# Graph layer with residual normalisation: single normalisation steps, the first x load on SyncE's queue, and evictions planned 0.3 later

## The chip, the cores and the metric

The kernel runs on one core of one Trainium2 chip. The metric is the device time of that core in microseconds; lower is better. Each kernel is executed several times and the median is taken. One more execution is recorded by the hardware profiler, and every duration of a single instruction below comes from that one.

## The reference, cut to what matters

There are 6250 nodes with 128 features and 100000 edges, sorted by destination. Every edge has one of two types. The layer multiplies the source node's features by the weights of the edge's type, sums over the edges that end in a node, adds the node's own product, applies relu, adds the input and normalises each row.

```python
Xs = X[src]
m_data = Xs @ W_data.T + b_data
m_ctrl = Xs @ W_control.T + b_control
msg = jnp.where((edge_types == 0)[:, None], m_data, m_ctrl)
agg = jax.ops.segment_sum(msg, dst, num_segments=X.shape[0])
out = agg + (X @ W_self.T + b_self)
h = x + relu(out)
result = (h - mean(h)) / sqrt(var(h) + 1e-5)      # along each row
```

## The kernel before, in words

The 6250 nodes are cut into 49 blocks of 128. In the first stage, called the y stage here, TensorE multiplies each block by both edge weights (the name y) and adds the bias with a second matmul. The result is kept as three bf16 parts, so that later bf16 matmuls lose nothing: ScalarE copies the first part out of PSUM into m3, TensorE subtracts it from y by a matmul with minus the identity, ScalarE copies the second part, and so on (the steps yh, y1, ym, y2, yl). The parts also go to a table in device memory. At the same time the edges of each destination block are loaded through a window that begins at the block's first edge. To find those first edges, VectorE compares the first destinations of rows of edges (r0, begun), GpSimd gathers one row per block (er), and TensorE turns the counts into a row (the matmul at L355), from which SyncE takes its addresses (first).

After that, 35 blocks are summed by matmuls and 14 by indirect gathers. For the 35, edges are put into slots by ranks (matmuls called tri and rest, reductions called slot, and the fill matmuls that write the tile small). The slots of a block go to device memory (packed) and come back broadcast to all partitions (rows); VectorE turns rows into one-hot matrices. Then, for each of 25 tiles of a block, four matmuls gather 128 edge messages into a PSUM tile g_ps (step g), ScalarE evicts it to gs in bf16 (step e), and four matmuls sum it into the block's agg with another one-hot matrix hot_d (step s). There are four g_ps buffers and eight gs buffers, so step g of a tile also waits for the eviction four tiles earlier. The last tile of a block goes to mixed, whose first rows come by an indirect gather. In the last group of blocks, VectorE may take an eviction instead of ScalarE. For the other 14 blocks, GpSimd gathers rows of the table (msg), and matmuls sum them with the one-hot matrix hot_g.

A finished block gets its own product (step o), relu, the residual and row statistics on VectorE. Blocks are then normalised in groups of up to five: VectorE and ScalarE compute scale and shift, and ScalarE applies them with one activation per block (L190, the function apply). The result is stored.

The order of all this on every engine is not left to the hardware. Each stage is a generator of steps; a step has a name, a cost for each engine that may run it, the names it needs, and a lag. The class Order runs them all against planned clocks, one per engine (T for TensorE, V, A, G and S for VectorE, ScalarE, GpSimd and SyncE). It picks the engine that can start first, and among the steps that could start there within 0.1 us the one with the earliest due time. A step's end is its start plus cost plus lag, and what needs it may start 0.25 later:

```python
self.free[engine] = start + costs[engine]
self.end[name] = start + costs[engine] + lag
```

The instructions are emitted in that order, and each engine runs its queue in order, with semaphores for what a step really needs. So costs, lags, due times and the initial clocks in order.free (L296) change no wait, only the order of the queues. The due times come from LEAD, BUILT, BLOCK and PACE (L383).

The head of the program, ahead of the planned steps, is written in a fixed order: the load of r0 on SyncE's queue, the loads of the bias and of w_sb on ScalarE's queue, constants, the bias split into three parts on VectorE (L271 to L274) and copied by ScalarE to bias3 (L276), then r0f and begun. A last branch, sums_over_all, is a fallback that is entered only if the windows missed edges.

Of the kernel before, what the change touches and what calls it, by code (L numbers as in the profile page):

```python
# [9 lines left out]
F32 = mybir.dt.float32  # L10
BF16 = mybir.dt.bfloat16
I32 = mybir.dt.int32
AF = mybir.ActivationFunctionType
# [6 lines left out]
P = 128  # L20
D = 128
D3 = 3 * D
# [29 lines left out]
PARTS = (4, 8, 8, 8, 8, 8, 5)  # L52
# [48 lines left out]
def step(name, costs, *needs, lag=0.0):  # L101
    return as_tuple(name), costs, [as_tuple(n) for n in needs], lag
# [6 lines left out]
@with_exitstack  # L109
def kernel(  # L110
    ctx: ExitStack,
    tc: tile.TileContext,
    x: bass.AP,
    xt: bass.AP,
    edges: bass.AP,
    w: bass.AP,
    bias: bass.AP,
    out: bass.AP,
):

    nc = tc.nc  # L140
    dram = ctx.enter_context(tc.tile_pool(name="dram", bufs=1, space=DRAM))
    const = ctx.enter_context(tc.tile_pool(name="const", bufs=1))
    table = dram.tile([NT * P, D3], BF16, name="table")
    packed = dram.tile([NPB, NT * R], BF16, name="packed")
    total = const.tile([1, 1], I32, name="total")

    def finish(h, agg, xs):

        nc.vector.scalar_tensor_tensor(h, agg, 0.0, xs, op0=ALU.max, op1=ALU.add)

    def add_parts(agg, work):
        whole = work.tile([P, D], F32, name="whole")
        nc.vector.tensor_reduce(whole, agg.rearrange("p (i c) -> p c i", i=3), axis=AX.X, op=ALU.add)  # L153
        return whole

    def load_rows(b, work, name="xs", bufs=2):
        xs = work.tile([P, D], F32, name=name, bufs=bufs)
        nc.sync.dma_start(xs, x[b * P : (b + 1) * P, :])
        return xs

    def stats(mv, h, work):
        st = work.tile([P, 6], F32, name="st")
        nc.vector.bn_stats(st, h)
        nc.vector.bn_aggr(mv, st)

    def root(mv, n, work):
        v = work.tile([P, Q], F32, name="v")
        nc.vector.tensor_scalar_add(v[:, :n], mv[:, :n, 1], EPS)
        s0 = work.tile([P, Q], F32, name="s0")
        nc.scalar.activation(s0[:, :n], v[:, :n], AF.Sqrt)  # L170
        return v, s0

    def scale(mv, v, s0, n, work):

        r0 = work.tile([P, Q], F32, name="r0")
        nc.vector.reciprocal(r0[:, :n], s0[:, :n])
        q = work.tile([P, Q], F32, name="q")
        nc.vector.tensor_mul(q[:, :n], v[:, :n], r0[:, :n])
        nc.vector.tensor_add(q[:, :n], q[:, :n], s0[:, :n])
        rstd = work.tile([P, Q], F32, name="rstd")  # L180
        nc.vector.reciprocal(rstd[:, :n], q[:, :n])
        nc.vector.tensor_scalar_mul(rstd[:, :n], rstd[:, :n], 2.0)
        shift = work.tile([P, Q], F32, name="shift")
        nc.vector.scalar_tensor_tensor(shift[:, :n], mv[:, :n, 0], -1.0, rstd[:, :n],
                                       op0=ALU.mult, op1=ALU.mult)
        return rstd, shift

    def apply(h, rstd, shift, n):
        for j in range(n):
            nc.scalar.activation(h[:, j, :], h[:, j, :], AF.Identity,  # L190
                                 bias=shift[:, j : j + 1], scale=rstd[:, j : j + 1])

    def store_out(h, b0, n, by=nc.sync):
        n0 = b0 * P
        full = min(n, (N - n0) // P)
        if full:
            by.dma_start(
                out[n0 : n0 + full * P, :].rearrange("(b p) f -> p b f", p=P), h[:, :full, :]
            )
        if full < n:  # L200
            n1 = n0 + full * P
            nc.sync.dma_start(out[n1:N, :], h[: N - n1, full, :])

    norm = stats, root, scale, apply, store_out

    with ExitStack() as main:
        sums_over_windows(main, tc, x, xt, edges, w, bias, table, packed, total,
                          add_parts, finish, load_rows, norm)

    matched = nc.values_load(total[0:1, 0:1])  # L210
    with tc.If(matched != E), ExitStack() as rest:
        sums_over_all(rest, tc, xt, edges, w, bias, table, dram, finish, load_rows, norm)


def sums_over_windows(ctx, tc, x, xt, edges, w, bias, table, packed, total,
# [21 lines left out]
    early = ctx.enter_context(ExitStack())  # L237
    build = early.enter_context(tc.tile_pool(name="build", bufs=2))
    ps_y = early.enter_context(tc.tile_pool(name="ps_y", bufs=YB, space=PSUM))
    b1 = build.tile([1, D3], F32, name="b1", bufs=1)  # L240
    A.dma_start(b1, bias)
    w_sb = const.tile([D, D3], F32, name="w_sb")
    A.dma_start(w_sb, w)


    iota_f = const.tile([P, 640], F32, name="iota_f")
# [46 lines left out]
        in_offset=bass.IndirectOffsetOnAxis(ap=row_i[:, 0:1], axis=0),  # L293
    )

    order.free.update(V=7.0, T=6.5, G=8.0)  # L296


    pid1 = const.tile([P, 1], F32, name="pid1")
# [74 lines left out]
            )  # L374


    xts, ys = {}, {}
    at_part = [sum(PARTS[:g]) for g in range(len(PARTS))]
    two_blocks = [(g, b, min(2, at_part[g] + n - b))
                  for g, n in enumerate(PARTS) for b in range(at_part[g], at_part[g] + n, 2)]  # L380


    LEAD, BUILT = 8.0, 76  # L383
    BLOCK = 13.1
    PACE = 1.68
    AHEAD, FIRST = 26.0, 20
# [60 lines left out]
    def load_x():  # L447
        for g, n in enumerate(PARTS):
            free = [("y", at_part[g - 1] - 1)] if g > 1 else []
            yield step(("xt", g), {"A": 0.45}, *free, lag=3.5)  # L450
            xts[g] = build.tile([D, max(PARTS), P], F32, name="xt")[:, :n]
            A.dma_start(xts[g].rearrange("p b c -> p (b c)"),
                        xt[:, at_part[g] * P : (at_part[g] + n) * P])

    def multiply():
        for i, (g, b, n) in enumerate(two_blocks):
            for j in range(n):
                free = [("yl", two_blocks[i - YB][1])] if i >= YB and j == 0 else []
                yield step(("y", b + j), {"T": 0.97}, ("xt", g), *free)
                if j == 0:  # L460
                    y = ys[b] = ps_y.tile([P, 2, 2 * D], F32, name="y")
                T.matmul(y[:, j, :], xts[g][:, b + j - at_part[g], :], w_sb[:, : 2 * D],  # L462
                         start=j == 0, stop=False, skip_group_check=True)
                T.matmul(y[:, j, :], ones_b, bias3[:, : 2 * D], start=False, stop=True, skip_group_check=True)  # L464
# [294 lines left out]
    def evict():  # L759
        for i, (b, g) in enumerate(tiles):  # L760
            free = [("s", *tiles[i - EB])] if i >= EB else []
            if g == NS - 1 and b:
                free.append(("s", b - 1, g))
            costs = {"A": 0.37, "V": 0.53} if b >= STARTS[-1] else {"A": 0.37}
            e = yield step(("e", b, g), costs, ("g", b, g), *free)
            if g < NS - 1:
                gs, at = late.tile([P, D3], BF16, name="gs", bufs=EB), slice(P)
            else:
                gs, at = mixed[blocks[b][0] % 2], slice(2 * R, P)
            gs_tiles[b, g] = gs  # L770
            (A.copy if e == "A" else V.tensor_copy)(gs[at], g_tiles.pop((b, g))[at, :D3])  # L771
# [19 lines left out]
    def own_of(blocks, begun):  # L791

        for i, b in enumerate(blocks):
            yield step(("agg", b), {"S": 0.0}, *([("whole", blocks[i - 1])] if i else []))
            yield step(("o", b), {"T": 0.5}, ("xs", b), begun(b))
            by_columns(aggs[b][:, :D], x_ts.pop(b), w_sb[:, 2 * D :], start=False, stop=False,
                       skip_group_check=True)
            by_columns(aggs[b][:, :D], ones_b, bias3[:, 2 * D :], start=False, stop=False,
                       skip_group_check=True)
# [16 lines left out]
    def normalise(pieces, last):  # L816

        for grp, (get, b0, q0, n) in enumerate(pieces):
            yield step((last, "root", grp), {"V": 0.2}, ("sum", b0 + n - 1))
            h, mv = get()  # L820
            h, mv = h[:, q0 : q0 + n, :], mv[:, q0 : q0 + n, :]
            v, s0 = root(mv, n, work)
            yield step((last, "rooted", grp), {"A": 0.3}, (last, "root", grp))
            yield step((last, "scale", grp), {"V": 1.0}, (last, "rooted", grp))
            scales = scale(mv, v, s0, n, work)
            yield step((last, "apply", grp), {"A": 0.28 * n}, (last, "scale", grp))
            apply(h, *scales, n)
            at_end = last == "p" and grp == len(pieces) - 1
            yield step((last, "out", grp), {"A": 0.4} if at_end else {"S": 0.3}, (last, "apply", grp))
            store_out(h, b0, n, nc.scalar if at_end else nc.sync)  # L830


# [99 lines left out]
def sums_over_all(ctx, tc, xt, edges, w, bias, table, dram, finish, load_rows, norm):  # L932
# [69 lines left out]
    for b0 in range(0, NB, Q):  # L1002
# [12 lines left out]
            finish(h[:, j, :], s_in, load_rows(b0 + j, work))  # L1015
            stats(mv[:, j, :], h[:, j, :], work)
        v, s0 = root(mv, n, work)
        apply(h, *scale(mv, v, s0, n, work), n)
        store_out(h, b0, n)


# [29 lines left out]
```

## Time and profile before

| What | Value |
|---|---|
| Median of 3 runs | 545.55 us (544.28 to 546.7) |
| The profiled execution | 628.27 us, its span 626.6 us |
| TensorE matmul busy | 550.4 us, 88% of the span |
| VectorE busy | 429.4 us, 69% |
| ScalarE busy | 424.7 us, 68% |
| GpSimd busy | 292.8 us, 47% |
| Mean granted TensorE clock | 0.985 |
| One eviction gs<-g_ps on ScalarE | 494 ns, 804 of them |
| One apply on ScalarE | 497 ns, 49 of them |

The profiled execution is slower than the runs without a profiler, so its durations and waits are compared with each other and with its own time. A line such as "PE agg L232 <- ACT gs L771" means that TensorE, at line 232, writing agg, sat idle until ScalarE's instruction at line 771 that wrote gs had ended. In a timeline line the first number is the start, the second the duration, both in us, then engine, line, operation, output and inputs, and in brackets the idle time before it and what ended it. "PE" is a matmul, "PEld" a weight load, "ACTq" and "SPq" are DMA issues in the queues of ScalarE and SyncE.

### The profile page before, as it was taken

The page shows a single profiled execution, that of the slowest core. Times are in us where ns is not written, and L with a number is a line of the kernel's source. Part 1 is how long each engine was busy: PE and PEld are TensorE (multiplying, and loading weights), DVE is VectorE, ACT ScalarE, POOL GpSimd, SP SyncE. Part 2 cuts the span into 40 slices and gives each one's busy share as a digit, 9 for nine tenths or more (in the row PEclk, how much of TensorE's full clock was granted, in tenths as well). Part 3 has the DMA queues.
Part 4 walks back from the last instruction along what each step waited for, and adds up shares of the span by engine and source line. Part 5 has one row for each costly group of instructions (what it writes and reads, how often), then busy time and mean ns, then how long its engine had stood idle before and what let it go on. Part 6 is the DMA issues. An engine that isn't in the chain of part 4 may idle for free.

```text
span 626.6 us, 26397 instructions
## 1 busy us (share of the span) xinstructions
PE 550.4 (88%) x11222; PEld 441.2 (70%) x11222; DVE 429.4 (69%) x962; ACT 424.7 (68%) x1008; POOL 292.8 (47%) x267
## 2 busy tenths in 40 slices
PE   5899888896989898897988989999999998888994
PEld 3555466675768686786877877788777787666783
DVE  4767677567667777776787766877686667446784
ACT  6755555565587666777767676786767876676684
POOL 1000026654465556655556464665646554554400
PEclk9999988999899999999999999999999999999998
DMA  3567754324243433435333433443344542534300
GB/s 108 168 196 221 249 188 128 117 66 158 58 127 123 127 111 117 136 109 152 93 128 114 142 122 106 127 144 106 122 133 119 157 152 68 161 103 146 106 18 27
DMA packets 60932, 79.19 MB, mean 126 GB/s; under 512 B 15760, under 2 KB 51371, under 8 KB 60807
## 3 DMA queue, kind: packets, MB, share of 16 engines
q1 hardware_dynamic: 47109, 48.88, 24.3%
q0 software_dynamic: 12400, 25.08, 14.3%
q10 hardware_dynamic: 1298, 3.48, 1.6%
q8 instruction: 89, 1.46, 0.9%
q14 instruction: 36, 0.29, 0.1%
HBM read 64.35 MB, written 13.05 MB: 124 GB/s over the span
## 4 chain that ended last, share of the span: by engine, by line
PE 80%; ACT 7%; issue 5%; DVE 4%; DMA 2%; SPq 1%; another core or an unknown queue 0%; POOL 0%; ACTq 0%; DVEq 0%; POOLq 0%
PE agg L232 27%; PE g_ps L756 26%; PE acc L232 8%; PE agg_g L232 8%; PE small L602 7%; ACT gs L771 5%; PE y L462 2%; ACT h_p L190 1%; DMA rows<-packed 1%; DVE slot L565 1%; PE y L480 1%; DVE hot_st L548 1%; ACT h_g L190 1%; PE y L464 0%; DMA xt<-in_xt 0%
## 5 line engine op out<-in xcount | busy, mean ns | idle before, releaser
L771 ACT CAST gs<-g_ps 128x384 bf16<-128x384 f32 x804 | 337.2, 494 | 151.3 <-PE g_ps L756 97.4
L857 POOL DMA_INDIRECT msg<-table,idx x252 | 283.1, 1124 | 208.0 <-PE g_ps L756 90.5
L756 PE MATMUL g_ps<-m,rows 128*32 128x384 bf16 x3430 | 330.8, 334 | 19.2 <-ACT gs L771 11.6
L232 PE MATMUL agg<-gs,hot_d 128*32 128x384 bf16 x3360 | 304.4, 338 | 27.8 <-ACT gs L771 12.9
L232 PEld LDWEIGHTS <-hot_d 128*32 128x32 bf16 x3500 | 198.9, 137 | 66.7 <-issue 56.4
L756 PEld LDWEIGHTS <-rows 128*32 128x32 bf16 x3430 | 185.5, 138 | 46.4 <-issue 40.6
L565 DVE TENSOR_REDUCE slot<-acc 128x5 bf16<-128x490 f32 x126 | 83.8, 665 | 75.5 <-PE acc L232 39.7
L232 PE MATMUL agg_g<-msg,hot_g 128*32 128x384 bf16 x1008 | 107.2, 330 | 1.2 <-issue 1.1
L741 DVE TENSOR_TENSOR hot_d<-count,to 128x1664 bf16<-128x1664 bf16 x70 | 74.7, 1068 | 21.7 <-PE agg L232 12.8
L602 PE MATMUL small<-hot_st,two 128*32 128x98 bf16 x1260 | 70.9, 290 | 1.4 <-issue 1.3
L602 PEld LDWEIGHTS <-two 128*32 128x32 bf16 x1260 | 56.8, 118 | 6.7 <-issue 4.6
L232 PE MATMUL acc<-hot_st,rest 128*32 128x490 bf16 x476 | 55.1, 380 | 6.1 <-DVE slot L565 5.0
L232 PE MATMUL acc<-hot_st,tri 128*32 128x490 bf16 x504 | 58.8, 376 | 1.0 <-DVE hot_st L548 0.9
L473 ACT CAST m<-y 128x512 bf16<-128x512 f32 (+1 forms) x75 | 40.6, 580 | 25.7 <-PE y L480 18.0
L232 PEld LDWEIGHTS <-hot_g 128*32 128x32 bf16 x1008 | 51.4, 125 | 4.9 <-issue 3.0
L548 DVE TENSOR_TENSOR hot_st<-count,st_b 128x2940 bf16<-128x2940 bf16 x21 | 41.9, 1997 | 13.7 <-PE small L602 5.4
L696 POOL DMA_INDIRECT mixed<-table,row_i x7 | 7.4, 1055 | 87.3 <-PE g_ps L756 81.2
L727 DVE TENSOR_SCALAR rows<-rows,pid 128x3136 bf16<-128x3136 bf16 x35 | 36.3, 1038 | 3.3 <-DMA rows<-packed 3.3
L153 DVE TENSOR_REDUCE whole<-agg 128x128 f32<-128x384 f32 x35 | 19.4, 553 | 27.5 <-PE g_ps L756 23.4
L462 PE MATMUL y<-w_sb,xt 128*128 128x256 f32 x98 | 31.6, 409 | 1.7 <-DMA xt<-in_xt 1.7
L232 PEld LDWEIGHTS <-rest 128*32 128x32 bf16 x476 | 20.9, 99 | 16.0 <-issue 15.3
L771 DVE CAST gs<-g_ps 128x384 bf16<-128x384 f32 x36 | 19.3, 554 | 13.7 <-PE g_ps L756 12.2
(140 smaller groups left out, 423.6 us busy)
## 6 DMA issues: line engine op xcount, KB each, us to landing
rows<-packed SPq DMA_DIRECT2D x35, 784.0 KB
table<-m SPq DMA_DIRECT2D x10, 768.0 KB
msg<-table,idx POOLq DMA_INDIRECT x252
xt<-in_xt ACTq DMA_DIRECT2D x5, 512.0 KB
xt_p<-in_xt SPq DMA_DIRECT2D x35, 64.0 KB
xs_p<-in_x SPq DMA_DIRECT2D x35, 64.0 KB
out<-h_p SPq DMA_DIRECT2D x6, 320.0 KB
table<-m SPq DMA_DIRECT2D x2, 480.0 KB
```

Source lines behind the costliest of these rows:

```text
L153: nc.vector.tensor_reduce(whole, agg.rearrange("p (i c) -> p c i", i=3), axis=AX.X, op=ALU.add)
L232: T.matmul(out[c : c + 32], lhsT[:, c : c + 32], rhs, **flags)
L462: T.matmul(y[:, j, :], xts[g][:, b + j - at_part[g], :], w_sb[:, : 2 * D], start=j == 0, stop=False, skip_group_check=True)
L473: A.copy(part_of(b, n, i), ys[b][:, :n, :].rearrange("p b (t c) -> p t b c", t=2))
L548: V.tensor_tensor(hot, counted[n][:, None, 1 : NT + 1, :].to_broadcast([P, KC, NT, n]), fields[grp][2][:, c * KC : c * KC + KC, None, :].t ...
L565: V.tensor_reduce(slots[grp][:, k, :], by_q, axis=AX.X, op=ALU.max)
L602: T.matmul(vt[c0 : c0 + R, q // 2, :], two[:, k % KC, i, :, q], hot[:, k % KC, :, q], start=k == 0 and q < 2, stop=k == KT - 1, skip_group ...
L727: V.tensor_scalar(rows[b], rows[b], pid1, None, op0=ALU.is_equal)
L741: V.tensor_tensor(hot, counted[DC][:, :, :n], places[grp][:, q, None, c * DC : c * DC + n].to_broadcast([P, P, n]), op=ALU.is_equal)
L756: T.matmul(g_ps[t * R : (t + 1) * R, :D3], rows[b][:, :, s], m3[:, s, :], start=True, stop=True)
L771: (A.copy if e == "A" else V.tensor_copy)(gs[at], g_tiles.pop((b, g))[at, :D3])
L857: G.indirect_dma_start(out=msgs[j, k], out_offset=None, in_=table[:, :], in_offset=bass.IndirectOffsetOnAxis(ap=idx[:, j, k : k + 1], axis=0),
```

## The change

The first part of x (xt, 128x512) is no longer loaded by a planned step on ScalarE's queue but by SyncE, straight after r0. On ScalarE's queue w_sb is now loaded ahead of the bias. The function apply does one block, and every block is a planned step of its own with a cost of 0.39 instead of 0.28 times the number of blocks. Evictions get a lag of 0.3. Three costs and two starting values of the plan change: y from 0.97 to 1.0, o from 0.5 to 0.25, TensorE's initial clock from 6.5 to 5.0, and LEAD from 8.0 to 6.0.

```diff
-    def apply(h, rstd, shift, n):
-        for j in range(n):
-            nc.scalar.activation(h[:, j, :], h[:, j, :], AF.Identity,
-                                 bias=shift[:, j : j + 1], scale=rstd[:, j : j + 1])
+    def apply(h, rstd, shift, j):
+        nc.scalar.activation(h[:, j, :], h[:, j, :], AF.Identity,
+                             bias=shift[:, j : j + 1], scale=rstd[:, j : j + 1])
...
+    w_sb = const.tile([D, D3], F32, name="w_sb")
+    A.dma_start(w_sb, w)
+    xts = {0: build.tile([D, max(PARTS), P], F32, name="xt")[:, : PARTS[0]]}
+    nc.sync.dma_start(xts[0].rearrange("p b c -> p (b c)"), xt[:, : PARTS[0] * P])
     b1 = build.tile([1, D3], F32, name="b1", bufs=1)
     A.dma_start(b1, bias)
-    w_sb = const.tile([D, D3], F32, name="w_sb")
-    A.dma_start(w_sb, w)
...
-    order.free.update(V=7.0, T=6.5, G=8.0)
+    order.free.update(V=7.0, T=5.0, G=8.0)
...
-    LEAD, BUILT = 8.0, 76
+    LEAD, BUILT = 6.0, 76
...
-            yield step(("xt", g), {"A": 0.45}, *free, lag=3.5)
+            yield step(("xt", g), {"A": 0.45} if g else {"S": 0.0}, *free, lag=3.5 if g else 0.0)
+            if not g:
+                continue
...
-                yield step(("y", b + j), {"T": 0.97}, ("xt", g), *free)
+                yield step(("y", b + j), {"T": 1.0}, ("xt", g), *free)
...
-            e = yield step(("e", b, g), costs, ("g", b, g), *free)
+            e = yield step(("e", b, g), costs, ("g", b, g), *free, lag=0.3)
...
-            yield step(("o", b), {"T": 0.5}, ("xs", b), begun(b))
+            yield step(("o", b), {"T": 0.25}, ("xs", b), begun(b))
...
-            yield step((last, "apply", grp), {"A": 0.28 * n}, (last, "scale", grp))
-            apply(h, *scales, n)
+            for j in range(n):
+                yield step((last, "apply", grp, j), {"A": 0.39}, (last, "scale", grp))
+                apply(h, *scales, j)
...
-            yield step((last, "out", grp), {"A": 0.4} if at_end else {"S": 0.3}, (last, "apply", grp))
+            yield step((last, "out", grp), {"A": 0.4} if at_end else {"S": 0.3}, (last, "apply", grp, n - 1))
```

In the fallback branch the call of apply becomes a loop over the blocks with the same instructions.

More of the change, by code (lines that the diff above doesn't have):

```diff
@@ L374, in starts @@
             )
-    xts, ys = {}, {}
+    ys = {}
     at_part = [sum(PARTS[:g]) for g in range(len(PARTS))]
@@ L1017, in sums_over_all @@
         v, s0 = root(mv, n, work)
-        apply(h, *scale(mv, v, s0, n, work), n)
+        scales = scale(mv, v, s0, n, work)
+        for j in range(n):
+            apply(h, *scales, j)
         store_out(h, b0, n)
```

## The prediction

> **What bounds the kernel now.** I read the page first: its busy shares and the chain of waits say which engine sets the end.
>
> ```profile
> span 626.6 us, 26397 instructions
> ...
> PE 550.4 (88%) x11222; PEld 441.2 (70%) x11222; DVE 429.4 (69%) x962; ACT 424.7 (68%) x1008; POOL 292.8 (47%) x267
> ...
> PE 80%; ACT 7%; issue 5%; DVE 4%; DMA 2%; SPq 1%; another core or an unknown queue 0%; POOL 0%; ACTq 0%; DVEq 0%; POOLq 0%
> ```
>
> TensorE is the bound: 88% busy and 80% of the chain. No matmul is added or removed, so only its idle time, 626.6 - 550.4 = 76 us in the profile, can change. The waits of TensorE come next (us in total, times, longest):
>
> ```profile
> PE agg L232 <- ACT gs L771: 12.9, 25, 1.8
> PE g_ps L756 <- ACT gs L771: 11.6, 18, 2.5
> ...
> PE acc L232 <- DVE slot L565: 5.0, 7, 1.4
> PE small L284 <- DVE begun L280: 4.9, 1, 4.9
> ```
>
> Evictions cost 24.5 us in 43 waits, the start 4.9 and another 1.7 for xt, the rank reductions 5.0. I then opened the timeline at three places. The start, 0 to 20 us:
>
> ```profile
> 2.24 0.34 DVE L271 CAST parts<-b 1x384 bf16<-1x384 f32 x1
> ...
> 7.00 1.19 PE L462 MATMUL y<-w_sb,xt 128*128 128x256 f32 x2 [1.75 <-DMA xt<-in_xt]
> ...
> 11.90 0.24 PE L355 MATMUL small<-ident,first_f 49*1 49x49 f32 x2
> ```
>
> Two chains begin here: the products y (first at 7.00), and bias parts (2.24), r0f (4.30), begun, gather of er (issued 5.94), first_f (9.88 to 10.03), L355 (11.90), first, windows (from 13.11), ranks. The handover from the y stage to the gathers, 75 to 80 us:
>
> ```profile
> 75.18 1.04 DVE L727 TENSOR_SCALAR rows<-rows,pid 128x3136 bf16<-128x3136 bf16 x1 [1.58 <-DMA rows<-packed]
> ...
> 77.54 1.04 DVE L727 TENSOR_SCALAR rows<-rows,pid 128x3136 bf16<-128x3136 bf16 x1 [0.75 <-DMA rows<-packed]
> ...
> 79.21 0.60 PE L232 MATMUL acc<-hot_st,rest 128*32 128x490 bf16 x4 [1.44 <-DVE slot L565]
> ```
>
> VectorE runs rows, slot, rows, slot in order; the second slot sits behind the second rows tile's load, and TensorE behind that slot; the first g follows at 79.98. Last, an apply block:
>
> ```profile
> 289.93 2.04 ACT L190 ACTIVATE h_g<-h_g,shift,rstd 128x128 f32<-128x128 f32 x5
> ...
> 292.38 0.39 PE L232 MATMUL agg<-gs,hot_d 128*32 128x384 bf16 x4 [0.83 <-ACT h_g L190]
> ```
>
> Five applies hold ScalarE for 2 us while evictions queue. The first wait of TensorE after such a block is 0.72 to 1.3 us in seven blocks (264.1, 292.4, 343.9, 417.8, 472.5, 497.2, 574.2): some 7 us of the 26 lost to ScalarE.
>
> **What the Trainium skill says.** "DMA: Bandwidth & Descriptors", section "Issuing engines are not separate DMA queues": issuing from several engines saves only sequencer time, since all run on the same 16 engines. That fits the start: the two xt issues take 0.82 us of ScalarE's queue, and they go out at 4.16 because three bias copies stand ahead. "TensorE: Matmul & The Clock Gate", Part 1: the array is at half speed until some 3.4 us of activity. The trace agrees: y pairs (product and bias) are 1.06 us apart until 10.1, then 0.54. "ScalarE: Activation LUTs", section "What ACT_TABLE_LOAD costs": neighbours overlap by about 93 ns. The trace has 497 ns for one apply and 2.04 us for five, so (2.04 - 0.50)/4 = 0.39 us each. The plan's old price, 0.28 x n, was too low; the new one, 0.39, is right.
>
> **The change part by part.** The compared queues hold the same 21,666 TensorE instructions in another order; VectorE gives six gs evictions to ScalarE and takes one mixed; SyncE gains the first xt load, ScalarE loses it.
>
> (1) Loads. Moving xt to SyncE puts it behind r0's issue (0.83 to 1.83) and ahead of the windows, which don't issue until 13.11, so it delays nothing there. It landed at about 7.0, 2.84 after its issue; from 1.83 that gives 4.7, or 5.2 shared with w_sb. The price: bias goes behind w_sb. It landed within 1.41 us of its issue (0.83 to 2.24); issued at 1.35 it lands by 2.8, by 3.5 if it trails w_sb's 192 KB. VectorE's four bias parts take 1.9 us and stand ahead of r0f, so r0f starts near 4.7 instead of 4.30: +0.4 (0 to +1.2) for begun, er and first_f (10.0 to 10.4). The first y moves from 7.00 to about 5.65, behind the begun matmuls (4.92 to 5.25, plus 0.4). L355 now stands behind six y and six correction matmuls, not five and two: the first three pairs start at 5.65, 6.7 and 7.75; then, from 8.2 when ScalarE's constant copies end, three rounds of eviction (0.6) and correction (0.3), in which the warm pairs (0.54) fit, and a last pair: 8.2 + 2.7 + 0.54, about 11.5 against 11.90. **Windows -0.4 us** (-1.0 to +3.0). The 1.35 us that y gains buys nothing by itself: the rank chain takes it up as a wait.
>
> (2) Handover. In the new VectorE order slot comes before the first rows, and the second rows follows two hot_d tiles. With rows landing as before at 75.2, rows ends 76.2, slot 76.9 to 77.5, hr and the two products (2.25 us) near 79.7 instead of 81.28. g can start near 77.5 instead of 79.98, but the 60 fills behind it need those products. **-1.6 us** (-2.5 to 0). What is late next is the first msg row: its gather is issued at 89.50, behind the table stores, and used at 92.72; the new order puts 20 more matmuls ahead of its use and takes two msgs together, so part may come back there.
>
> (3) lag=0.3, with the repriced y, o, T and LEAD. These only reorder. Counting from the queues, one gather or sum (four matmuls) every 0.16 us (starts 612.18, 612.34, 612.50): a g_ps buffer is reused within five such steps of its gather 52 times before and 30 after, of 871; a gs tile is summed that soon 10 times, then 11. An eviction is 494 ns plus the 0.39 of its gather, so about five steps is where it must wait. Scaling the 11.6 us of g_ps waits by 22/52 gives -4.9, at most, since a removed wait leaves ScalarE as far behind; nothing for the 12.9. I take **-1.5**, lower bound -4.9, upper +1.5 for new tight places.
>
> (4) Single applies. Four of the ten multi-row blocks are broken up (1+4 twice; 1+1+1+1 and 1+3 at the end); six stay five long. TensorE work between a gather and its sum, for the first tile behind each of the first seven of these blocks, goes (us) 1.74, 1.70, 2.12, 1.86, 1.91, 2.45, 1.95 to 1.95, 1.87, 1.95, 2.28, 1.32, 2.12, 1.57. The fifth and seventh fall, but there one apply (0.39) stands ahead instead of five (2.0); the third and sixth fall a little, though the sixth's g_ps buffer is reused after 2.28, not 1.41. Roughly 3.5 us of cover against 7 of waits: **-2** (-3.5 to 0).
>
> (5) Six gs moved to ScalarE: 6 x 0.395 = 2.4 us of its time after 560 us, where it is busy 28.08 of 40, then 13.39 of 15. TensorE covers it (14.76 of 15); without that cover it is late. **+0.3** (0 to +1). The fallback branch's loop has no instruction in the trace: nothing. The tail, from the last sum at 617.4, is unchanged.
>
> Sum in the profiled execution: -0.4 - 1.6 - 1.5 - 2 + 0.3 = -5.2, so 628.27 (span 626.6 and 1.7 around it) becomes 623.1. The median of the runs, 545.55, is 83 us shorter, so waits on ScalarE are smaller there. The first two terms are loads and VectorE work and I keep them; I cut (3) to -0.8 and (4) to -1.5: -0.4 - 1.6 - 0.8 - 1.5 + 0.3 = **-4.0, 541.5 us**.
>
> **The rivals.** *Nothing measurable.* Orders change, waits move: msg at 92.7 takes back the handover, evictions stay as tight for sums (10 to 11). For it: ScalarE's backlog isn't removed. Against: the seven apply waits are real. About 545 (543 to 548). *Slower, by the start.* Bias lands behind w_sb at 3.5, L355 waits for three rounds of ScalarE evictions, and the windows come 3 us late; everything to the first g hangs on them. It decides from about 1.6 us of delay, when the handover is eaten; with half of the upper ends of (3), (4) and (5), 0.5 x (1.5 + 0 + 1), it gives 545.55 + 3.0 - 1.6 + 1.25 = 548.2. For it: first_f waits on that chain, and L355 was already 1.9 us late. Against: TensorE starts y 1.35 us earlier.
>
> **How the numbers follow.** 0.5% is 2.73 us, about what a measurement of this kernel can tell from no change (its three runs span 544.28 to 546.7). The forecast has 0.55, the first rival 0.24, the second 0.21. Its own range is 538 to 542.8; with the rivals 537 to 548.5.
>
> **What would show it.** Right: first y near 5.7, L355 near 11.5, first g_ps near 77.5, TensorE's waits on gs well under 24.5, waits after apply blocks near 0.5. Wrong: parts after 3.2, L355 past 13, rows landing later than 75.2, a new wait on msg above 2 us, or as many waits on gs as before.

## The result, and the profile after

Over 20 runs of each, the changed kernel takes 543.71 us (541.36 to 547.27) and the kernel before 545.74 (544.15 to 549.32). The ratio is **0.9959, 95% interval 0.9940 to 0.9977**: 2.2 us faster. The prediction was 541.5, 4.0 us faster, with a range of its own of 538 to 542.8 and of 537 to 548.5 with its rivals: the measured time is just above the first and inside the second.

The first thing to read in the profile after is its own time: 542.47 us, near the median of its runs. The profile shown of the kernel before took 628.27, 83 us above its median. All times here depend on the chip: the same program takes some 546 us on one chip and 630 to 637 us on two others. The profile before looks like one from a chip of the second kind. Its time is one that the kernel before has there, and its idle times for which the trace shows no releaser (called "issue") are of that size: 24.5 us for matmuls and 142.8 for weight loads, where the eight profiles taken at 630 and 637 us have 22.0 to 36.8 and 135.6 to 161.9, and the five taken at 546 us have 0 to 0.9 and 58.5 to 67.0. So the profiler need not be what made it slow, as the text ahead of the prediction supposes: the changed kernel was profiled too, without loss. I therefore compare the changed kernel with a second profile of the kernel before (experiment 1, 548.74 us). The page of the changed kernel, in the order of the lines shown of before (span, busy times, the chain by engine):

```profile
span 540.7 us, 26393 instructions
...
PE 506.7 (94%) x11222; PEld 437.1 (81%) x11222; DVE 425.3 (79%) x957; ACT 421.9 (78%) x1013; POOL 293.8 (54%) x267
...
PE 75%; DVE 11%; DMA 8%; issue 2%; ACT 2%; SPq 1%; POOL 0%; ACTq 0%; DVEq 0%; POOLq 0%
```

The second profile of the kernel before has:

```profile
span 547.0 us, 26397 instructions
...
PE 507.0 (93%) x11222; PEld 440.1 (80%) x11222; DVE 427.1 (78%) x962; ACT 420.3 (77%) x1008; POOL 296.4 (54%) x267
```

The 11222 matmuls are the same, but they keep TensorE busy for 507.0 us here, not 550.4, so that difference is not made by the change. The changed kernel is idle for 34.0 us of its span, the kernel before for 40.0. The waits of TensorE in the changed kernel (us in total, times, longest):

```profile
PE agg_g L231 <- DMA msg<-table,idx: 8.8, 8, 1.9
PE small L285 <- DVE begun L281: 5.7, 1, 5.7
PE acc L231 <- DVE slot L568: 5.0, 12, 0.9
PE agg L231 <- ACT gs L774: 1.5, 4, 0.6
```

The waits for evictions, 24.5 us in the first profile of before, are 1.5 here, or 2.1 with the two evictions by VectorE. But the waits of the kernel before in its second profile show that most of that fall is not due to the change:

```profile
PE agg_g L232 <- DMA msg<-table,idx: 8.7, 7, 3.5
PE acc L232 <- DVE slot L565: 6.3, 9, 1.9
PE agg L232 <- ACT gs L771: 5.0, 11, 0.9
PE small L284 <- DVE begun L280: 4.9, 1, 4.9
PE y L462 <- DMA xt<-in_xt: 1.8, 1, 1.8
PE acc L232 <- DVE hot_st L548: 1.2, 1, 1.2
PE agg L232 <- DVE gs L771: 1.0, 2, 0.7
PE g_ps L756 <- ACT gs L771: 0.9, 2, 0.6
```

At this speed the kernel before waits 6.9 us for evictions (5.0 + 1.0 + 0.9). The longest wait is for gathered rows, which the first profile does not list for TensorE. The start and the handover of the changed kernel, from its timeline (start, duration, instruction, idle time before it):

```profile
3.29 0.35 DVE L272 CAST parts<-b 1x384 bf16<-1x384 f32 x1 [0.97 <-DMA b<-in_bias]
...
5.98 1.22 PE L465 MATMUL y<-w_sb,xt 128*128 128x256 f32 x2
...
12.24 0.24 PE L356 MATMUL small<-ident,first_f 49*1 49x49 f32 x2
...
76.65 1.03 DVE L730 TENSOR_SCALAR rows<-rows,pid 128x3136 bf16<-128x3136 bf16 x1
...
76.79 0.39 PE L231 MATMUL acc<-hot_st,rest 128*32 128x490 bf16 x4 [0.15 <-DVE slot L568]
...
78.31 0.39 PE L231 MATMUL acc<-hot_st,rest 128*32 128x490 bf16 x4 [0.62 <-DVE slot L568]
...
78.72 0.83 PE L759 MATMUL g_ps<-m,rows 128*32 128x384 bf16 x16
```

The bias parts wait for the bias and begin 1.05 us later than before (2.24); y begins 1.02 earlier; the matmul of first_f stands at 12.24. The first rows tile no longer waits for its load, and TensorE waits 0.15 and 0.62 us for slot. In the kernel before, second profile, its first two rows tiles wait 1.90 and 1.25 us for their loads (the second is shown), and the same places are:

```profile
12.62 0.24 PE L355 MATMUL small<-ident,first_f 49*1 49x49 f32 x2
...
77.97 0.39 PE L232 MATMUL acc<-hot_st,rest 128*32 128x490 bf16 x4 [1.68 <-DVE slot L565]
...
79.17 1.04 DVE L727 TENSOR_SCALAR rows<-rows,pid 128x3136 bf16<-128x3136 bf16 x1 [1.25 <-DMA rows<-packed]
...
80.84 0.60 PE L232 MATMUL acc<-hot_st,rest 128*32 128x490 bf16 x4 [1.94 <-DVE slot L565]
...
81.60 1.52 PE L756 MATMUL g_ps<-m,rows 128*32 128x384 bf16 x16
```

The first g_ps moved from 81.60 to 78.72, by 2.88 us, and the two waits for slot ahead of it are 2.85 us shorter. A count of TensorE's progress compares the executions further on; it is the start, in us, of the 490th, 980th and so on of the 3430 g_ps matmuls:

| kernel (its profiled time) | 490 | 980 | 1470 | 1960 | 2450 | 2940 | 3430 |
|---|---|---|---|---|---|---|---|
| before, second profile (548.74) | 154.9 | 222.1 | 289.4 | 354.6 | 421.2 | 485.0 | 538.0 |
| changed (542.47) | 151.5 | 219.6 | 286.4 | 351.1 | 416.5 | 477.8 | 530.8 |
| head alone (547.62) | 149.5 | 217.9 | 286.1 | 353.7 | 420.8 | 484.0 | 536.4 |

The changed kernel is 3.4 us ahead at 490, 2.5 to 3.5 ahead up to 1960, and 7.2 ahead at the end. These are single executions, 6.3 us apart where the medians are some 2 apart, so about two thirds of the lead at the end cannot be put down to the change.

### The profile page after: what moved, and what is told of

It reads as the page before. It is cut to its first block, busy times and chain, and to the rows that moved or that the text cites. A ratio compares the mean times of both kernels' runs of the same rounds, so it can differ in the third digit from the quotient of the medians.

```text
span 540.7 us, 26393 instructions
## 1 busy us (share of the span) xinstructions
PE 506.7 (94%) x11222; PEld 437.1 (81%) x11222; DVE 425.3 (79%) x957; ACT 421.9 (78%) x1013; POOL 293.8 (54%) x267
## 4 chain that ended last, share of the span: by engine, by line
PE 75%; DVE 11%; DMA 8%; issue 2%; ACT 2%; SPq 1%; POOL 0%; ACTq 0%; DVEq 0%; POOLq 0%
PE agg L231 25%; PE g_ps L759 22%; PE acc L231 9%; PE small L605 7%; PE agg_g L231 7%; DMA msg<-table,idx 6%; DVE slot L568 2%; DVE hot_st L551 2%; PE y L465 2%; DMA rows<-packed 1%; PE y L483 1%; ACT gs L774 1%; DVE two L589 1%; ACT h_p L189 1%; DVE whole L153 0%
## 5 line engine op out<-in xcount | busy, mean ns | idle before, releaser
L759 PE MATMUL g_ps<-m,rows 128*32 128x384 bf16 x3430 | 319.3, 331 | 0.0
L231 PE MATMUL agg<-gs,hot_d 128*32 128x384 bf16 x3360 | 297.9, 330 | 2.6 <-ACT gs L774 1.5
L231 PEld LDWEIGHTS <-hot_d 128*32 128x32 bf16 x3500 | 187.9, 137 | 15.4 <-issue 7.9
L605 PE MATMUL small<-hot_st,two 128*32 128x98 bf16 x1260 | 72.0, 291 | 0.6 <-DVE two L589 0.6
L231 PEld LDWEIGHTS <-hot_g 128*32 128x32 bf16 x1008 | 52.8, 123 | 15.8 <-issue 12.4
L231 PE MATMUL acc<-hot_st,tri 128*32 128x490 bf16 x504 | 60.8, 375 | 1.5 <-DVE hot_st L551 1.5
L605 PEld LDWEIGHTS <-two 128*32 128x32 bf16 x1260 | 58.6, 117 | 4.3 <-issue 1.5
L231 PEld LDWEIGHTS <-rest 128*32 128x32 bf16 x476 | 22.3, 98 | 14.9 <-issue 13.4
L231 PEld LDWEIGHTS <-tri 128*32 128x32 bf16 x504 | 21.5, 99 | 3.9 <-issue 3.4
```

The costliest lines, as they stand in the source:

```text
L231: T.matmul(out[c : c + 32], lhsT[:, c : c + 32], rhs, **flags)
L605: T.matmul(vt[c0 : c0 + R, q // 2, :], two[:, k % KC, i, :, q], hot[:, k % KC, :, q], start=k == 0 and q < 2, stop=k == KT - 1, skip_group ...
L759: T.matmul(g_ps[t * R : (t + 1) * R, :D3], rows[b][:, :, s], m3[:, s, :], start=True, stop=True)
```

## The experiments

All ratios are to the kernel before on the same chip, with a 95% interval. Where a chip of 630 to 637 us is named, the ratios hold for that kind of chip alone.

**1. The kernel before again** (no edit), chip at 546 us.

> The kernel before, unchanged, profiled again. Its first profile ran 628 us, 83 us above its median, while the changed kernel's ran 542 us, at its median: the two traces don't compare. Theory A (the recorded steps: waits for evictions shrank): in a profile near 546 us TensorE waits 8 to 12 us in total for gs, after apply blocks above all, and the first g_ps stands near 80. Theory B (those waits were made by the slowed execution): the waits for gs are under 3 us, as in the changed kernel (1.5), and the 2.2 us that were gained lie elsewhere. Timed against itself, the ratio is 1.000 within 0.2%.

Ratio 1.0011 (0.9987 to 1.0035). The profile is the one shown above. Waits for gs are 6.9 us, between what the two theories said. So the first profile had overstated them by 3.6 times for a chip at 546 us, but they are not nil. Theory A was right about the place: each of the ten groups of applies is followed by one wait of TensorE for ScalarE's gs (0.23 to 0.86 us), 5.2 us together of the 5.9 that ScalarE causes. The first of them, and below it one of the four in the changed kernel:

```profile
166.28 2.03 ACT L190 ACTIVATE h_p<-h_p,shift,rstd 128x128 f32<-128x128 f32 x5
...
168.73 0.39 PE L232 MATMUL agg<-gs,hot_d 128*32 128x384 bf16 x4 [0.86 <-ACT gs L771]
```

```profile
297.44 2.04 ACT L189 ACTIVATE h_p<-h_p,shift,rstd 128x128 f32<-128x128 f32 x5
...
299.89 0.39 PE L231 MATMUL agg<-gs,hot_d 128*32 128x384 bf16 x4 [0.28 <-ACT gs L774]
```

**2 to 4. One part alone**, same chip and same runs of before.

```diff
-            e = yield step(("e", b, g), costs, ("g", b, g), *free)
+            e = yield step(("e", b, g), costs, ("g", b, g), *free, lag=0.3)
```

> Only lag=0.3 on the evictions, everything else as before. Theory A: about 0.8 us faster (0.15%), waits on gs lower than in the kernel before. Theory B: no change beyond 0.1%, or either sign by another order of the queues; waits on gs small in both.

The head alone:

```diff
+    xts = {0: build.tile([D, max(PARTS), P], F32, name="xt")[:, : PARTS[0]]}
+    nc.sync.dma_start(xts[0].rearrange("p b c -> p (b c)"), xt[:, : PARTS[0] * P])
...
-    order.free.update(V=7.0, T=6.5, G=8.0)
+    order.free.update(V=7.0, T=5.0, G=8.0)
...
-    LEAD, BUILT = 8.0, 76
+    LEAD, BUILT = 6.0, 76
```

(with w_sb loaded ahead of the bias, and no planned load of the first xt).

> Only the head: first xt on SyncE's queue, w_sb ahead of the bias, T=5.0, LEAD=6.0. Theory A: windows about unchanged (L355 between 11.5 and 12.3), first g_ps 1 to 2 us earlier through the new order of VectorE's slot and rows, so 1 to 2 us faster. Theory B: the same first g_ps, but the first msg (landing at 92.8 in the changed kernel) takes it back: under 0.7 us faster.

The single applies alone:

```diff
-            yield step((last, "apply", grp), {"A": 0.28 * n}, (last, "scale", grp))
-            apply(h, *scales, n)
+            for j in range(n):
+                yield step((last, "apply", grp, j), {"A": 0.39}, (last, "scale", grp))
+                apply(h, *scales, j)
```

> Only the single applies at 0.39 each. Theory A: 1.5 us faster (0.27%), no wait of TensorE above 0.5 us after an apply block. Theory B: no change within 0.15%: at normal speed TensorE had no wait after apply blocks.

| part | ratio | TensorE's waits for gs | first g_ps | TensorE busy, idle |
|---|---|---|---|---|
| none (experiment 1) | 1.0011 (0.9987 to 1.0035) | 6.9 | 81.60 | 507.0, 40.0 |
| lag | 0.9991 (0.9972 to 1.0011) | 2.7 | 81.09 | 503.3, 37.4 |
| head | 1.0015 (0.9994 to 1.0036) | 6.3 | 77.84 | 506.5, 39.4 |
| applies | 1.0016 (0.9994 to 1.0038) | 3.3 | 80.54 | 510.6, 36.8 |
| all of the change | 0.9959 (0.9940 to 0.9977) | 2.1 | 78.72 | 506.7, 34.0 |

The ratio of the whole is that of the result above. It was timed then, beside runs of the kernel before of its own, and not again with the parts. The last three columns are of one profiled execution each. In these, each part does what it was said to do: with lag or applies there are fewer waits for gs, and the head brings the first g_ps 3.8 us forward. None of them alone gives a gain that can be measured. The intervals rule out the 1.5 us of theory A for the applies and its 1 to 2 us for the head; for lag they leave both theories standing. With the applies alone, waits of 0.69 and 0.58 us still follow groups of applies, so both theories were wrong about them: A said none above 0.5, B none in the kernel before.

A wait that goes need not be time that is won. The profile of the applies alone has 3.2 us less idle time than that of the kernel before and 3.6 us more busy time, for the same matmuls. Its granted clock is 0.986, the others' 0.992 to 0.994. The busy times of these five executions lie 7.3 us apart, more than what is being sought. The execution with lag alone (542.39 us) is also the fastest of its 14 runs, whose median is 546.45.

With the head alone the first gathered product shows what comes next:

```profile
77.84 0.83 PE L760 MATMUL g_ps<-m,rows 128*32 128x384 bf16 x16
...
94.91 0.84 PE L232 MATMUL agg_g<-msg,hot_g 128*32 128x384 bf16 x8 [4.73 <-DMA msg<-table,idx]
```

TensorE reaches the product early and waits 4.73 us for the row. That wait doesn't eat the lead, since the kernel before waits there too (1.98, 0.42 and 3.46): in the table of progress the head is 5.4 us ahead at 490. It is 3.3 ahead at 1470, 0.4 at 2450 and 1.1 at the end of the execution, so in these two executions the lead fades in the long stage of gathers and sums. Why it fades is not shown; TensorE's waits for gs are 6.3 us with the head alone and 6.9 in the kernel before.

**5 to 8. The change without one part, and two variants**, on a chip at 637 us.

Without lag=0.3:

> The changed kernel without lag=0.3 on the evictions. The profile of the kernel before, taken again at normal speed, has 5.9 us of waits of TensorE for ScalarE's gs, not 24.5; the changed kernel has 1.5, and lag alone on the kernel before had 1.8. Theory A (lag removes these waits and is most of the gain): gs waits back to 4 to 6 us, 0.2 to 0.4% slower than the changed kernel, about the time of the kernel before. Theory B (the gain is the handover and the head): 0.996 of the kernel before, as the whole change.

Without the head (the edit of experiment 3 undone in the changed kernel):

> The changed kernel with the old loads, T=6.5 and LEAD=8.0. Theory A (the handover is taken back by the first msg, lag is the gain): first g_ps after 80.5, first msg product still near 93 to 94.5, and about 0.997 of the kernel before. Theory B (the handover is the gain): ratio 1.000, 2 us slower than the whole change.

Gathered rows planned 3 us later:

```diff
-            yield step(("msg", j, k), {"G": PACE}, *free, lag=3.0 - PACE)
+            yield step(("msg", j, k), {"G": PACE}, *free, lag=6.0 - PACE)
```

> The changed kernel, with gathered rows planned as landing 3 us later (lag 6.0 - PACE instead of 3.0 - PACE), which puts each msg product some 40 matmuls (1.6 us) later in TensorE's queue. It tests what the changed kernel still loses: 8.8 us of waits of TensorE for msg, 4.6 of them for the first products at 92.8 to 101.7. Theory A (the handover's gain is lost to these waits): waits for msg under 4 us and 2 to 4 us faster than the changed kernel, ratio to the kernel before 0.989 to 0.993. Theory B (the gathers on GpSimd's queue set the pace, with five msg buffers that come free later): waits move elsewhere, 0.995 to 0.999.

The bias issued ahead of w_sb again:

```diff
+    b1 = build.tile([1, D3], F32, name="b1", bufs=1)
+    A.dma_start(b1, bias)
     w_sb = const.tile([D, D3], F32, name="w_sb")
     A.dma_start(w_sb, w)
...
-    b1 = build.tile([1, D3], F32, name="b1", bufs=1)
-    A.dma_start(b1, bias)
```

> The changed kernel with the bias issued ahead of w_sb again; xt stays on SyncE's queue. In the changed kernel the bias parts began at 3.29 instead of 2.24, and first_f's matmul stood at 12.24 instead of 11.90 to 12.62. Theory A: parts at 2.24, begun 0.8 us earlier, first_f's matmul between 11.3 and 12, first g_ps 0.3 to 0.8 us earlier, but 0 to 0.5 us in the time, since the first msg is bound by the table stores. Theory B (the bias order is a cost of its own): 0.8 to 1 us faster than the changed kernel.

Measured: without lag 1.0058 (1.0038 to 1.0078), without the head 1.0227 (1.0194 to 1.0259), rows later 0.9945 (0.9923 to 0.9966), bias first 1.0109 (1.0075 to 1.0143). The kernel before took 636.76 us here, so these numbers do not sort out the 2.2 us won at 546. TensorE waits 15.5 to 21.2 us for ScalarE's gs in all four, least of all without the lag. With the bias first, the parts begin at 2.24, first_f's matmul stands at 11.71 and the first g_ps at 78.30, as expected; its effect on the time at 546 us stays open.

**9 and 10. The changed kernel and the later rows together**, on another chip, at 630 us.

> The changed kernel, again. The four runs before this one were on a chip where the kernel before takes 637 us, and TensorE idles some 30 us for nothing the profile shows (issue); the whole change was measured where it takes 546. Theory A: the change is worth the same 0.4% on any chip, ratio 0.994 to 0.998. Theory B: on a chip at 637 us the order that fits is another one, since the kernel with the bias first, nearly the same queues, was 1.1% slower there: ratio 1.005 to 1.015 if this call lands on such a chip, 0.994 to 0.998 if it lands on one at 546.

> The changed kernel with the gathered rows planned 3 us later, beside the changed kernel on the same chip. Theory A (the handover's gain is lost to the first msg products): on a chip at 546 us waits for msg fall from 8.8 us to under 4 and it is 2 to 4 us faster than the changed kernel (0.4 to 0.7%); at 637 us it is faster too, as its 0.9945 suggests. Theory B (the gathers set the pace): within 0.2% of the changed kernel.

**11 and 12. Later rows and no head once more.** They landed on the chip of experiments 5 to 8, at 637 us.

> The changed kernel with the gathered rows planned 3 us later, a third time. It was 0.55% and 0.79% faster than the kernel before on chips at 637 and 630 us, where the changed kernel was 1.6% slower. Theory A (the handover's gain is lost to the first msg products): on a chip at 546 us waits for msg fall from 8.8 us to under 4, ratio 0.989 to 0.993, below the changed kernel's 0.996. Theory B (at 546 us the gathers set the pace): 0.995 to 0.998.

> The changed kernel with the old loads, T=6.5 and LEAD=8.0, again; at 637 us it was 2.3% slower than the kernel before. On a chip at 546 us, theory A (the handover is taken back by the first msg): first g_ps 1.5 to 3 us later than the changed kernel's 78.7, ratio 0.995 to 0.998 all the same. Theory B (the head is the gain): 1.000 to 1.004. On a slower chip: 1.02 again.

On the chip at 630 us the whole change is slower, **1.0156 (1.0125 to 1.0188)**; the later rows are faster in all three trials, 0.9945, 0.9921 (0.9893 to 0.9949) and 0.9925 (0.9906 to 0.9945); without the head it is 1.0244 (1.0220 to 1.0268). Beside each other on the chip at 630 us, the changed kernel takes 640.45 us and the one with the later rows 625.74. So the sign of this change was not the same on the two chips on which it was timed, as theory B of experiment 9 said. Here the changed kernel has waits of TensorE that its page at 546 us lacks:

```profile
PE 559.3 (88%) x11222; PEld 441.4 (69%) x11222; DVE 427.7 (67%) x957; ACT 426.4 (67%) x1013; POOL 286.0 (45%) x267
...
PE agg L231 <- issue: 18.1, 47, 1.0
PE g_ps L759 <- issue: 11.3, 26, 1.6
PE agg L231 <- ACT gs L774: 8.9, 18, 1.0
```

and with the rows later, on the same chip:

```profile
PE g_ps L759 <- ACT gs L774: 9.8, 16, 1.7
PE agg L231 <- ACT gs L774: 9.4, 18, 1.2
PE g_ps L759 <- issue: 9.3, 19, 1.2
...
PE agg L231 <- issue: 6.2, 16, 0.9
```

Beside the first profile of the kernel before, which looks like one of such a chip, the changed kernel waits less for ScalarE's gs, 14.6 us instead of 24.5. Yet its span is 9.1 us longer (635.7 and 626.6): TensorE is busy for 8.9 us more (559.3 and 550.4), and "issue" is 8.8 us more (33.3 and 24.5).

Theory A of experiment 7 (0.989 to 0.993) was right in its number in two of the three trials and wrong in its reason. The changed kernel's first two gathered products wait only 1.45 us for rows here (0.52 and 0.93), and the later rows do not shrink the waits for gs, which grow. What shrinks is "issue", from 33.3 to 22.0 us over all lines, and the busy time, from 559.3 to 552.8. At 637 us, where the changed kernel itself was not run, "issue" is 31.5 and 29.4 with the later rows. Why a few steps of distance make the kernel faster was not found. At 546 us the later rows were not tried, since the chips of the later runs were all slower ones.

## Why the prediction was right or wrong

The side was right, and the time lies in the wide range (541.5 forecast, 543.7 measured). But the gain is about half of the forecast, the time is above the forecast's own range of 538 to 542.8 and inside that of the rival "nothing measurable" (543 to 548), and the runs do not confirm the sum that it came from. That the forecast came this near is in part luck.

**What can change.** The prediction said that with the same matmuls only TensorE's idle time can change. In the traces the busy time of the same 11222 matmuls is 503.3 to 510.6 us at 546 us, and 550.4 to 561.5 in the first profile and those at 630 and 637. So a change in waits cannot simply be subtracted from the time.

**Loads (-0.4).** The bias was the delay that was priced: the parts began at 3.29, near the upper end (3.5), not 2.8. The first y was right (5.98 for 5.65). The matmul of first_f was forecast at 11.5 and stands at 12.24, where the kernel before has 11.90 and 12.62 in its two profiles. The head alone has 11.80. So the term is nil within what these profiles tell. Of the recorded signs of being wrong, one came, parts after 3.2, at no cost that can be seen. The rival that the start comes 3 us late did not happen at this speed.

**Handover (-1.6).** The mechanism is shown: with slot ahead of rows, TensorE's last two waits for slot ahead of the first g_ps are 0.15 and 0.62 us instead of 1.68 and 1.94. With the head alone they are 0.15 and 1.07, with lag or the applies alone still 3.1 and 3.5 together. The first g_ps was forecast at 77.5 and came at 78.72, 2.9 us ahead of the second profile of before and 1.3 ahead of the first; rows began at 76.65, not 75.2, because slot in front of it began at 76.06. With the head alone it came at 77.84. But what it is worth in the end is not the 1.6 of the sum: alone, the head is 1.0015 with an interval that ends at 0.9994, at best 0.3 us.

**Evictions and applies (-0.8 and -1.5).** These terms were mis-sized: they were scaled from 24.5 us of waits in a profile that ran 83 us above its median. The prediction saw the 83 us and cut the terms by a third; at the speed of the runs the whole of these waits is 6.9 us, so the cut should have been to under a third. The direction is confirmed for the waits: lag alone leaves 2.7, applies alone 3.3, the whole 2.1. But alone they are worth 0.9991 and 1.0016, within noise of nothing, though the traces have 4.2 and 3.6 us of waits less. Term (4) rested on seven waits after apply blocks, given as 0.72 to 1.3 us (the timeline has 0.78 to 1.32); in the second profile no wait of TensorE's sums for gs is over 0.9. Their place was right: all of the changed kernel's 1.5 us still follow groups of applies (0.28 to 0.57), near the 0.5 that was forecast. But of the 3.7 us by which these waits fell from 5.2, 2.9 are behind the six groups that stay five long and 0.8 behind the four that are broken up. So most of the fall is the new order of the queues around the applies, not their breaking up.

**Six evictions on ScalarE (+0.3).** ScalarE does 810 instead of 804, VectorE 30. TensorE's last group of matmuls begins at 531.87 in the changed kernel. From its end to the end of the span are 8.4 us, where the kernel before has 7.7 and 8.8 in its two profiles. No cost of the move can be seen.

**The rival "nothing measurable"** is close: 2.2 us is inside its 0.5% band, and 543.7 in its range, though the interval of the ratio ends short of 1. Its reason, that msg takes the handover back, is not what was seen: both kernels wait 8.7 to 8.8 us for rows.

What stays open: which part of the change carries the 2.2 us at 546 us. No part alone reaches it in these timings, whose intervals are about 1 us to either side. The new prices of y and o were in no part, so they may carry some of it; and since whole and parts were timed apart, some of the difference may come from that. The two runs that were to show it by taking one part away landed on a chip at 637 us. There, versions that differ only in the order of the queues lie between 0.9925 and 1.0244, several times the size of the effect. Whether the parts add up to the whole was not tested on any chip with enough precision to say.

## What to carry to other kernels

Compare the profiled execution's own time with the median before sizing anything by its waits: here it was 15% longer, and the waits that it showed were 3.6 times those at the speed of the runs. Where engines run fixed queues against each other, a change of order can do in the trace what it says (a wait goes, a step comes forward) and still win no time that can be measured, as the parts alone did here. A gain of 0.4% from reordering is a fact about the chips it was measured on; the same version lost 1.6% on another.

## What the runs showed of the hardware that was not expected

The same program takes 545.74 us in the first measurement and 630.21 or 636.76 on two other chips, with nearly the same durations of single instructions. In the changed kernel an eviction takes 497 ns at 546 us and 493 at 630, a g_ps matmul 331 and 335, and the granted clock is 0.992 and 0.985. Its span is 95.0 us longer at 630 us (635.7 against 540.7). Of these, 42.4 are idle time of TensorE (76.4 against 34.0), for which the trace shows no releaser in 33.3 us ("issue") against none at 546. The larger part, 52.6 us, is busy time. The profile counts time in which matmuls overlap once, so matmuls of the same length that follow each other less closely make a longer busy time: the 3430 g_ps matmuls cover 319.3 us at 546 and 337.8 at 630. The "issue" waits of the weight loads go the same way, 67.0 us in the kernel before and 58.5 in the changed kernel at 546, against 148.7 at 630. The cause was not found.
